# A two-layer graph network in Strassen-Winograd form: taller bank fills, smaller first sums, P2's first steps ahead of P6, and more of the next P1 inside the first aggregation

## The chip, the cores and the metric

The kernel runs on one core of a Trainium2 chip, in float32. The metric is the device time of one execution in microseconds (us): 1880.43 us, the median of three runs (1879.48 to 1881.2). One further execution was profiled; its span is 1878.8 us. The engines are called by the profile's names: PE is TensorE (PEld its weight loads), DVE VectorE, ACT ScalarE, POOL GpSimd, SP the engine that starts the DMAs.

## The reference

There are 64 graphs of N = 256 nodes with F = 512 features, a dense adjacency matrix for each, and weights that all graphs share.

```python
# layer 0
deg = sum(adj, -1);  agg = (adj @ x) / max(deg, 1e-6)
x1  = layernorm(x + relu(concat([x, agg], 2) @ W.T))
# layer 1
q, k = split(x1 @ Wqk);  v = x1 @ Wv
w   = inv_scale * mask * rowsum(q * (adj @ (k * mask)))
out = layernorm(x1 + softmax(w over nodes) * v)
```

In layer 1 the two halves of Wqk are multiplied with each other once, at the start, since rowsum(q * (adj @ k)) can be written as a row sum of (x1 @ (Wq Wk^T)) * (adj @ x1). So each layer is one product of the features with a 512 x 1024 weight and one product of an adjacency with a 256 x 512 matrix.

## The kernel before

**Pairs and layers.** Graphs are handled two at a time (index k), in 32 pairs. Loop index j runs over the pairs; iteration j holds layer 0 of pair j and layer 1 of pair j-1, written into each other. For iteration 0 there is no layer 1, and a tail after the loop does layer 1 of the last pair.

**Winograd's form of Strassen's product.** A feature-by-weight product is cut into 2 x 2 blocks and done with seven products instead of eight: P1 to P7, on sums S1 to S4 of the left blocks and T1 to T4 of the weight blocks. P4, P6 and P7 are plain products of 512 columns (`outer`, `pairs`); P1, P2, P3 and P5 are cut once more (`inner`), into seven products of 256 columns. `inner` returns four units: `first_two`, `second`, `third`, `last_two`. Their products share a working bank `w`: the upper half holds the fifth product, the lower half is accumulated on, and between products ScalarE copies what has been reached so far into the result banks. So `second` starts with a product onto `lo`, which `first_two` has accumulated and which `act.copy(q[0][:, :HF], lo)` has to read before. P1 and P2 use one working bank (`pw[0]`), P5 and P3 the other (`pw[1]`). P1 and P6 share the result banks `u`: when P1's four units are done, VectorE adds the fifth product to both banks, `after_p1` has ScalarE copy both to `own`, and P6 then accumulates on top in the same banks.

**Aggregation.** `gather` does the adjacency product as seven block products for both graphs, as units named a to g, on sums of adjacency blocks (`sa`, by GpSimd) and of feature blocks (`tv`, by VectorE).

**What sets the order.** Nothing is reordered later: matmuls, DMAs and the calls on VectorE, ScalarE and GpSimd go out in the order in which the program makes them. The order of the matmuls is written out by hand, in strings such as `run("i k i k", i=i, k=k)`; every letter takes the next unit of its list. In layer 0, i is P1, k is P5, m is P2, p is P6, q is P7, r is P3 and s is P4. After most units `tick()` looks at chains of queued vector and scalar steps (degrees, norms, softmax, weight sums) and issues those that are due by a small cost model: `mm` adds 0.43 or 0.86 us to a clock, and each engine has an estimate of when it is free.

**Start.** Eight products of a constant `ones` write each of the eight banks once (`fill`). Then follow 16 products for Wq Wk^T, while the weights and the first pair's features land, VectorE forms the weight sums and GpSimd the first `inner_sums`.

In the profile nearly all matmuls have line L175 (`mm`), all vector, scalar and GpSimd calls L90 (`InOrder`), all DMA starts L180; they are told apart by their tiles. `xT` holds layer 0's features turned, `xT_s` and `xT_i` their outer and inner sums, `x1T` those of layer 1; `t`, `t_i` and `w` are weight sums and weights; `bank` is a PSUM bank.

Of the kernel before, what the change touches and what calls it, by code (L numbers as in the profile page):

```python
# [36 lines left out]
BF16 = mybir.dt.bfloat16  # L37
# [4 lines left out]
P = 128  # L42
# [5 lines left out]
S1, S2, S3, S4 = range(4)  # L48
# [46 lines left out]
def resnorm_kernel(  # L95
# [13 lines left out]
    B, N, F = x.shape  # L109
# [8 lines left out]
    const = ctx.enter_context(tc.tile_pool(name="const", bufs=1))  # L118
# [49 lines left out]
    def run(order, **units):  # L168
        for name in order.split():
            units[name].pop(0)()  # L170
# [63 lines left out]
    wide = [const.tile([P, Q], F32, name=f"wide{k}") for k in (0, 1)]  # L234
    for w in wide:
        vec.memset(w, 0.0)
    ones = const.tile([1, P], BF16, name="ones")
    vec.memset(ones, 1.0)

    def fill(pair):  # L240
        for k in range(2):
            mm(pair[k].rearrange("p (a n) -> p a n", n=P), ones,
               ones[:, None, :].to_broadcast([1, F // P, P]), start=True)
    for pair in banks:
        fill(pair)

    def weight_product(c, ps):
# [49 lines left out]
    def inner_sums(X, eng, part):  # L297

        if X.s is None:
            X.open_sums()  # L300
        of_sum = lambda n: lambda k, e: X.s[:, k, X.slot[n]:X.slot[n] + 1, e]
        ks, b = ((slice(0, 2), X.first_row), (slice(2, 3), of_sum(S1)), (slice(0, 1), of_sum(S4)))[part]
        a11, a12, a21, a22 = (b(k, e) for k in range(2) for e in range(2))
        i = [X.i[:, r, ks] for r in range(4)]
        for to, op, c, d in ((i[0], OP.add, a21, a22), (i[1], OP.subtract, i[0], a11),
                             (i[2], OP.subtract, a11, a21), (i[3], OP.subtract, a12, i[1])):
            eng.tensor_tensor(to, c, d, op=op)
# [435 lines left out]
    for part in (work[:5], [sums[0][1]], work[5:10], [sums[1][1]], work[11:16]):  # L743
        for do in part:
            do()
    inner_sums(Xs[0], gp, 0)
    inner_sums(Xs[0], gp, 1)
    sumsA[0] = adj_sums(0)
    degrees(0)
    vec.free = clock[0] + 5.5  # L750
# [6 lines left out]
    early = []  # L757

    for j in range(NP):
        X = Xs.pop(j)  # L760
        if j == 2:
            steady.append(True)
        flush("finish")
        owns[j] = pool.tile([P, 2, NT, F], F32, name="own", bufs=3)
        if j > 0:
            load_adj(j)
            run_now(late_sums)
            late_sums.clear()
            sumsA[j] = adj_sums(j)

        u, y, o = pf, py, pu
        ys[j] = pool.tile([P, 2, NT, F], F32, name="y")
        a1, a2, a3, a4, a5, a6, a7 = layer0(j, o, u, y)
        i = inner("P1", X, W0, pw[0], u, a1)
        k = inner("P5", X, W0, pw[1], y, a5)
        m = inner("P2", X, W0, pw[0], o, a2)
        p, q = pairs(u, X, S2, W0["T2"], a6), pairs(u, X, S3, W0["T3"], a7)
        r, s = inner("P3", X, W0, pw[1], y, a3), pairs(u, X, A22, W0["T4"], a4)
        if j == 0:
            run("i k i k i k i k", i=i, k=k)  # L780
            flush("degrees")
            load_rows(1)
        elif j == 1:
            early.append(a1)
            run("k i k m k i k", i=early[0], k=k, m=m)
            fourth_sums(X, [1])
            run("m p p", m=m, p=p)
            fourth_sums(X, [0])
            run("p p m", m=m, p=p)
            load_x(1)  # L790
        else:
            run("i k", i=i, k=k)
            send_scores(j - 2)
            run("i l k", i=i, k=k, l=open1)
            flush("norm")
            fetch_scores(j - 2)
            places[0](range(16))
            run("i k i k", i=i, k=k)
        if j != 1:
            fourth_sums(X, [1])  # L800
        if j > 1:
            flush("mask")
            sumsM[j - 1] = adj_sums(j - 1)
            if j + 1 < NP:
                load_rows(j + 1)
            load_x(j)
        if j > 1:
            softmax(j - 2)
            shared[0] = 1.0
        if j != 1:  # L810
            run("m p p", m=m, p=p)
            fourth_sums(X, [0])
            run("m p p m", m=m, p=p)
        flush("w0a")
        run("q q q", q=q)
        flush("w0")
        run("r q r m", m=m, q=q, r=r)
        if j == 1:
            flush("norm")
        quiet[0] = j < 2  # L820
        room[vec] = -9.0 if j > 1 else 0.6
        run("r s r", r=r, s=s)
        if j > 0:
            Y = x1Ts.pop(j - 1)
        if j > 1:
            inner_sums(Y, gp, 0)
            queue(1, "sums", *outer_sums(Y, vec), (vec, lambda Y=Y: inner_sums(Y, gp, 1)))
        T_late = []
        T = sums_T(ys[j], T_late, 0 if j < 2 else 1)

        if j == 0:
            degrees(1)
        zs[j] = pool.tile([P, 2, NT, HF], F32, name="z")
        g = gather(sumsA.pop(j), T, zs[j], pw[1], y[1], y[0], owns[j], rdegs[j], T_late)

        def sums_next():
            if j == NP - 1:
                return
            inner_sums(Xs[j + 1], gp, 0)
            rest = outer_sums(Xs[j + 1], gp)  # L840
            run_now(rest[:1])
            inner_sums(Xs[j + 1], gp, 1)
            late_sums.extend(rest[1:])
        if j == 0:
            sums_next()
            held = [c for c in chains if c[1] == "w1"]
            chains[:] = [c for c in chains if c[1] != "w1"]
            early.append(inner("P1", Xs[1], W0, pw[0], u, lambda fifth: early[1](fifth)))
            run("s s a b s c d i e i g f", s=s, i=early[0], **g)
            quiet[0] = False  # L850
        else:
            u2, o2, y2 = o, pf, y
            b1, b2, b3, b4, b5, b6, b7, b8 = layer1(j - 1, ys[j][:, :, 0], o2, u2, y2)
            jj = inner("P1", Y, W1, pw[0], u2)
            k = inner("P2", Y, W1, y[0], o2, b2)
            if j == 1:
                turn_here(Y, owns[0], 0, pw)
                flush("mask")
                sumsM[0] = adj_sums(0)
                load_rows(2)  # L860
                run("s", s=s)
                turn_here(Y, owns[0], 1, pw)
                inner_sums(Y, gp, 0)
                sums_Y = (*outer_sums(Y, vec), (vec, lambda: inner_sums(Y, gp, 1)))
                run("s a b s d c", s=s, **g)
                quiet[0] = False
                flush("w1")
                run("e j g f", j=jj, **g)
                queue(1, "sums", *sums_Y)
                run("k j k j k j", j=jj, k=k)  # L870
                b1(None)
                run("k", k=k)
            else:
                run("s s j s a b", s=s, j=jj, k=k, **g)
                room[vec] = 0.6
                run("j", j=jj)
                if j < NP - 1:
                    degrees(j + 1)
                run("c d j k e j", s=s, j=jj, k=k, **g)
                quiet[0] = True  # L880
                run("k", k=k)
                quiet[0] = False
                b1(None)
                run("g f", **g)
        flush("softmax", "adds", "sums", "degrees")
        if j > 0:
            aggs[j - 1] = late.tile([P, 2 * N_SIDE], F32, name="agg").rearrange(
                "p (k t f) -> p k t f", k=2, t=NT)
            vs[j - 1] = [late.tile([P, NT, F], F32, name="v", bufs=2) for _ in range(2)]
            T = sums_T(owns[j - 1])  # L890
            g = gather(sumsM.pop(j - 1), T, aggs[j - 1], pw[0], o2[1], o2[0])
            h, q = pairs(u2, Y, S2, W1["T2"], b6), pairs(u2, Y, S3, W1["T3"], b7)
            n = inner("P5", Y, W1, pw[1], y2, b5)
            p, open1 = pairs(u2, Y, A22, W1["T4"], b4), inner("P3", Y, W1, pw[1], y2, b3)
            norm0(j)
            mask_adj(j)
            run("k h h" if j > 1 else "h h", k=k, h=h)
            if j == 1:
                degrees(2)
                flush("degrees")  # L900
            if j < NP - 1:
                load_xT(j + 1)
            run("n k h h" if j > 1 else "n h h", k=k, n=n, h=h)
            fourth_sums(Y)
            shared[0] = 1.25
            sums_next()
            run("a n b q d q n c q e q n p g f", n=n, q=q, p=p, **g)
            b8()
            run("p l p l p l", p=p, l=open1)
            py, pu = pu, py  # L910
        else:
            norm0(0)
            mask_adj(0)
            chains.extend(held)
# [113 lines left out]
```

## Time and profile before

| what | value |
|---|---|
| median of three runs | 1880.43 us |
| profiled span | 1878.8 us |
| PEld busy | 1314.0 us (70%) |
| POOL busy | 909.2 us (48%) |
| DMA | 181.27 MB, mean 96 GB/s |
| matmul 128x512, typical row | 592 ns |
| matmul 128x256, typical row | 380 ns |
| ACT copy of 128x256, 128x512 | 377, 583 ns |

The busy time of an engine is the union of its instructions' times. A float32 matmul shows as two records. Rows of consecutive matmuls overlap[...]; the distance between starts, and not a row's length, is what a matmul costs. In a timeline row the numbers are the start and the length in us; "x4" joins four like records, and "[0.26 <-X]" means that the engine was idle for 0.26 us before, and that X is inferred to have ended it.

### The profile page before, as it was taken

What the parts mean: (1) busy time and instruction counts of PE and PEld (TensorE: products, weight loads), DVE (VectorE), ACT (ScalarE), POOL (GpSimd) and SP (SyncE); (2) the same over time, 40 slices, a digit from 0 to 9 for tenths busy, and PEclk for the clock granted to TensorE, in tenths of its full rate; (3) what the DMA queues carried; (4) which work ended last, traced back from release to release, by engine and by line L of the source; (5) the groups of instructions that cost most, each with busy time, mean ns of one, the idle gap of its engine ahead of it and who ended that gap; (6) DMA issues with size and microseconds to landing.
All of it is one profiled execution on the core that took longest, in us unless ns stands there. A gap on an engine that the chain in (4) does not pass through costs nothing.

```text
span 1878.8 us, 25005 instructions
## 1 busy us (share of the span) xinstructions
PE 1859.2 (99%) x7000; PEld 1314.0 (70%) x7000; DVE 1511.1 (80%) x3180; ACT 1309.1 (70%) x3274; POOL 909.2 (48%) x1251
## 2 busy tenths in 40 slices
PE   9999999999999999999999999999999999999997
PEld 5667777767777677677677777776776777776765
DVE  6787888778887778887778887788877788877887
ACT  3667776677777677767777766777676777767766
POOL 4455443555444554535554535554445544355532
PEclk9999999999999999999999999999999999999999
DMA  6123334333333433343333334333434233433321
GB/s 225 57 69 82 100 94 113 90 90 96 107 97 88 114 82 99 90 118 85 100 91 103 96 98 106 85 99 96 110 85 113 80 103 94 110 94 86 99 64 51
DMA packets 380714, 181.27 MB, mean 96 GB/s; under 512 B 263712, under 2 KB 345248, under 8 KB 380576
## 3 DMA queue, kind: packets, MB, share of 16 engines
q1 hardware_dynamic: 380576, 179.67, 35.4%
q8 instruction: 57, 0.93, 0.2%
q14 instruction: 81, 0.66, 0.1%
HBM read 114.10 MB, written 34.06 MB: 79 GB/s over the span
## 4 chain that ended last, share of the span: by engine, by line
PE 96%; DVE 2%; ACT 1%; DMA 0%; issue 0%; POOL 0%; DVEq 0%; ACTq 0%
PE bank L175 96%; ACT own L90 1%; DVE v L90 0%; DVE own L90 0%; ACT bank L90 0%; DVE turn L90 0%; DMA wqk<-wqk_t 0%; DVE tv L90 0%; DVE y L90 0%; PE bank L628 0%; POOL xT_s L90 0%; DVE bank L90 0%; POOL sa L90 0%; ACT x1T L90 0%; DVE st L90 0%
## 5 line engine op out<-in xcount | busy, mean ns | idle before, releaser
L90 ACT COPY bank<-bank 128x256 f32<-128x256 f32 (+1 forms) x768 | 332.3, 435 | 235.8 <-PE bank L175 224.7
L90 DVE TENSOR_TENSOR y<-bank,y 128x512 f32<-128x512 f32 x256 | 170.5, 686 | 131.9 <-ACT y L90 131.3
L90 ACT ACTIVATE own<-own,shift,rstd 128x512 f32<-128x512 f32 x255 | 199.8, 808 | 0.9 <-DVE shift L90 0.9
L175 PE MATMUL bank<-tv,sa 128*128 128x256 f32 x768 | 192.5, 380 | 1.0 <-DVE tv L90 0.9
L90 POOL TENSOR_TENSOR x1T_s<-x1T,x1T_s 128x256 f32<-128x256 f32 x64 | 63.6, 1013 | 267.7 <-PE bank L175 267.7
L90 POOL TENSOR_TENSOR x1T_i<-x1T_s 128x128 f32<-128x128 f32 x128 | 101.1, 790 | 182.8 <-DVE x1T_s L90 182.8
L90 ACT ACTIVATE junk<-own,less 128x512 bf16<-128x512 f32 x254 | 183.7, 723 | 3.0 <-DVE less L90 2.1
L175 PEld LDWEIGHTS bank<-tv,sa 128*128 128x128 f32 x768 | 145.4, 190 | 49.9 <-issue 23.1
L90 ACT COPY y<-bank 128x512 f32<-128x512 f32 x192 | 108.8, 583 | 95.2 <-PE bank L175 93.7
L90 POOL TENSOR_TENSOR sa<-adj 128x256 f32<-128x256 f32 x128 | 94.7, 740 | 165.9 <-DMA adj<-adj_t 152.1
L175 PE MATMUL bank<-w,x1T_s 128*128 128x512 f32 (+1 forms) x384 | 168.3, 521 | 0.0
L90 POOL TENSOR_TENSOR x1T_i<-x1T 128x256 f32<-128x256 f32 x64 | 55.4, 866 | 221.6 <-DMA x1T<-turn 209.0
L175 PE MATMUL bank<-t,xT_s 128*128 128x512 f32 (+1 forms) x384 | 159.3, 524 | 2.5 <-ACT own L90 1.5
L175 PE MATMUL bank<-t,x1T_s 128*128 128x512 f32 (+1 forms) x384 | 158.1, 521 | 0.3 <-ACT y L90 0.3
L90 DVE TENSOR_TENSOR v<-bank,v 128x512 f32<-128x512 f32 x186 | 119.2, 682 | 48.8 <-PE bank L175 48.8
L175 PE MATMUL bank<-w,xT_s 128*128 128x512 f32 (+1 forms) x384 | 153.1, 521 | 0.0
L175 PE MATMUL bank<-t_i,xT_i 128*128 128x256 f32 x512 | 152.7, 380 | 0.3 <-DVE own L90 0.2
L175 PE MATMUL bank<-t_i,x1T_i 128*128 128x256 f32 x512 | 152.2, 379 | 0.1
L175 PEld LDWEIGHTS bank<-t_i,x1T_i 128*128 128x128 f32 x512 | 97.1, 190 | 67.1 <-issue 48.6
L175 PEld LDWEIGHTS bank<-t_i,xT_i 128*128 128x128 f32 x512 | 94.6, 189 | 58.2 <-issue 45.7
L90 ACT COPY own<-bank 128x512 f32<-128x512 f32 x128 | 71.8, 587 | 89.9 <-PE bank L175 49.3
L175 PE MATMUL bank<-t,x1T 128*128 128x512 f32 x256 | 130.4, 592 | 0.0
(159 smaller groups left out, 4565.6 us busy)
## 6 DMA issues: line engine op xcount, KB each, us to landing
x<-x SPq DMA_DIRECT2D x64, 512.0 KB, 5.7
xT<-x_t SPq DMA_DIRECT2D x62, 512.0 KB, 5.5
out<-own SPq DMA_DIRECT2D x62, 512.0 KB, 3.2
x1T<-turn SPq DMA_DIRECT2D x480, 64.0 KB, 2.3
adj<-adj_t SPq DMA_DIRECT2D x64, 256.0 KB, 3.8
turn<-adj SPq DMA_DIRECT2D x64, 256.0 KB, 3.0
row<-d SPq DMA_DIRECT2D x31, 256.0 KB, 4.7
wqk<-wqk_t SPq DMA_DIRECT2D x4, 512.0 KB, 5.7
```

The costliest lines, as they stand in the source:

```text
L90: return self.tc.keep_in_program_order(getattr(self.engine, name)(out, *args, **kwargs))
L175: tc.keep_in_program_order(nc.tensor.matmul(ps, a, b, start=start, stop=True, skip_group_check=True))
```

## The change

Five edits:

- The constant has 128 rows instead of one, so the fill products contract over all 128 rows, and the first two banks are filled twice: ten products instead of eight.
- `inner_sums` learns two more parts: those of P1 and of P2 alone. At the start GpSimd forms P1's sums, then P5's, then P2's, where it formed P1's and P2's together and then P5's.
- In layer 0 of pair 0 and of pairs 2 to 31, P2's first unit moves ahead of P5's last, and P2's second comes before P6 begins, its third between P6's two halves: from `i k i k i k i k | m p p | m p p m` to `i k i k i k i m k | m p p | m p p`.
- Three units of pair 1's P1, instead of two, run inside pair 0's aggregation; pair 1's own order changes to `k i k m k p k | p m | p p m`.
- In pair 1's iteration, aggregation unit b comes before a.

```diff
-    ones = const.tile([1, P], BF16, name="ones")
+    ones = const.tile([P, P], BF16, name="ones")
     vec.memset(ones, 1.0)
 
     def fill(pair):
         for k in range(2):
             mm(pair[k].rearrange("p (a n) -> p a n", n=P), ones,
-               ones[:, None, :].to_broadcast([1, F // P, P]), start=True)
-    for pair in banks:
+               ones[:, None, :].to_broadcast([P, F // P, P]), start=True)
+    for pair in (banks[0], *banks):
         fill(pair)
...
-        ks, b = ((slice(0, 2), X.first_row), (slice(2, 3), of_sum(S1)), (slice(0, 1), of_sum(S4)))[part]
+        ks, b = ((slice(0, 2), X.first_row), (slice(2, 3), of_sum(S1)), (slice(0, 1), of_sum(S4)),
+                 *((slice(v, v + 1), lambda k, e, v=v: X.first_row(k, e)[:, v:v + 1]) for v in range(2)))[part]
...
-    inner_sums(Xs[0], gp, 0)
-    inner_sums(Xs[0], gp, 1)
+    for part in (3, 1, 4):
+        inner_sums(Xs[0], gp, part)
...
         if j == 0:
-            run("i k i k i k i k", i=i, k=k)
+            run("i k i k i k i m k", i=i, k=k, m=m)
             flush("degrees")
             load_rows(1)
         elif j == 1:
             early.append(a1)
-            run("k i k m k i k", i=early[0], k=k, m=m)
+            run("k i k m k p k", i=early[0], k=k, m=m, p=p)
             fourth_sums(X, [1])
-            run("m p p", m=m, p=p)
+            run("p m", m=m, p=p)
             fourth_sums(X, [0])
             run("p p m", m=m, p=p)
...
-            run("i k i k", i=i, k=k)
+            run("i k i m k", i=i, k=k, m=m)
...
         if j != 1:
             run("m p p", m=m, p=p)
             fourth_sums(X, [0])
-            run("m p p m", m=m, p=p)
+            run("m p p", m=m, p=p)
...
-            run("s s a b s c d i e i g f", s=s, i=early[0], **g)
+            run("s s a b s c i d i e i g f", s=s, i=early[0], **g)
...
-                run("s a b s d c", s=s, **g)
+                run("s b a s d c", s=s, **g)
```

## The prediction

> **What bounds the kernel now.** I read the page first (busy shares and the chain that ended last), then the chain in order of time to find where it leaves TensorE, then the timeline around those places.
>
> ```profile
> PE 1859.2 (99%) x7000; PEld 1314.0 (70%) x7000; DVE 1511.1 (80%) x3180; ACT 1309.1 (70%) x3274; POOL 909.2 (48%) x1251
> PE 96%; DVE 2%; ACT 1%; DMA 0%; issue 0%; POOL 0%; DVEq 0%; ACTq 0%
> ```
>
> TensorE is 99% busy and 96% of the chain. All of its matmuls stay in the changed kernel, so a change can only move the time that TensorE stands still. That time comes from start-to-start distances: undisturbed, a 256-column record follows after 0.215 us and a 512-column one after 0.43 us, and whatever is longer is lost. Outside the first 95 us nothing much is lost. Two pairs show the place that the change rearranges in all 30 pairs from the third on. Columns are start, length, engine, line, operation, out<-in, shape, count.
>
> ```profile
> 1093.16 1.30 DVE L90 STREAM_TRANSPOSE turn<-own 128x512 f32<-128x512 f32 x2
> ...
> 1094.38 1.40 DVE L90 TENSOR_TENSOR bank<-bank,fifth 128x256 f32<-128x256 f32 x4
> ...
> 1094.69 0.59 PE L175 MATMUL bank<-w,xT 128*128 128x256 f32 x2
> ...
> 1094.82 1.07 ACT L90 COPY own<-bank 128x512 f32<-128x512 f32 x2 [1.65 <-DVE bank L90]
> ...
> 1095.55 1.95 PE L175 MATMUL bank<-t,xT_s 128*128 128x512 f32 x4 [0.26 <-POOL sa L90]
> ...
> 1095.77 0.39 ACT L90 COPY bank<-bank 128x256 f32<-128x256 f32 x1
> ```
>
> ```profile
> 350.69 1.50 DVE L90 TENSOR_TENSOR bank<-bank,fifth 128x256 f32<-128x256 f32 x4
> ...
> 351.12 1.07 ACT L90 COPY own<-bank 128x512 f32<-128x512 f32 x2 [1.07 <-DVE bank L90]
> ...
> 351.58 0.59 PE L175 MATMUL bank<-w,xT 128*128 128x256 f32 x2
> ...
> 352.01 1.88 PE L175 MATMUL bank<-t,xT_s 128*128 128x512 f32 x4
> ...
> 352.21 0.36 ACT L90 COPY bank<-bank 128x256 f32<-128x256 f32 x1
> ```
>
> When P1 ends, VectorE adds the fifth product to P1's two banks, ScalarE copies both banks to own, and P6 (t,xT_s, 512 columns) may then accumulate in the first of them. The releaser printed for P6 is POOL, but those subtractions do not touch its operands; the own copy, 0.15 us after whose end P6 starts, is what it needs. Its undisturbed start is 0.43 us after the row "w,xT", so 1094.69+0.43 = 1095.12, and 0.43 us are lost. In the second pair it starts on time. Over the 30 pairs, 14 lose 0.08 to 0.43 us, 3.8 us together, and the record after a wait comes 0.075 us late each time (14 x 0.075 = 1.05): 4.8 us in all. That is the most that hiding P6's wait can bring.
>
> The start and the first two pairs:
>
> ```profile
> 1.15 3.59 PE L175 MATMUL bank<-ones 1*128 1x512 bf16 x8 [1.15 <-DVE ones L90]
> 5.22 1.22 PE L175 MATMUL bank<-wqk 128*128 128x512 f32 x1 [0.47 <-DMA wqk<-wqk_t]
> 9.65 0.34 PEld L175 LDWEIGHTS bank<-wqk 128*128 128x128 f32 x1 [0.52 <-issue]
> 10.50 0.20 PEld L175 LDWEIGHTS bank<-wqk 128*128 128x128 f32 x1 [0.52 <-issue]
> 10.95 0.19 PEld L175 LDWEIGHTS bank<-wqk 128*128 128x128 f32 x1 [0.24 <-issue]
> 48.36 1.13 PE L175 MATMUL bank<-tv,sa 128*128 128x256 f32 x4 [0.90 <-DVE tv L90]
> 61.63 1.10 PE L175 MATMUL bank<-t,xT_s 128*128 128x512 f32 x2 [0.82 <-ACT own L90]
> 79.29 1.99 PE L175 MATMUL bank<-y,adj 128*128 128x256 f32 x8 [0.78 <-ACT x1T L90]
> ```
>
> Until 10.5 us the weight products come 0.85 us apart, afterwards 0.43 us apart: TensorE runs at half speed, although the clock column says full.
>
> **What the Trainium skill says.** "TensorE: Matmul & The Clock Gate", section "What's actually happening", has the array at half clock by default and at full clock after about 3.4 us of sustained activity, in windows that do not start with the kernel. The trace agrees on the factor (0.85 against 0.43 us); that eight one-row products over 3.6 us did not release the clock fits, but whether for their height or the pause of 0.47 us after them no run here shows. The same page, "LDWEIGHTS (loading the stationary operand)", makes the load's time depend on columns, not rows, so taller fill products cost nothing each. "PSUM — Partial Sum Buffer", section "Engine vs sequencer instructions", says that ScalarE and VectorE queues are strict FIFO and matmuls run in program order; in both pairs above ScalarE takes own, own, bank in issue order.
>
> **The change, part by part.**
>
> *Fill.* Two more products, all with 128 rows. Cold fill products stand 0.43 us apart, so ten last from 1.15 to 5.42 us and the first weight product moves from 5.22 to about 5.4: 0.2 us lost. TensorE is then active without a break from 1.15 us. If a clock window counts that was not counted before, the step at 10.5 us comes 3.4 us (the skill's window) earlier, and half of it is gained: 1.7. Ends: a loss of 0.2 if height and pause don't matter, a gain of 2.4 if all six slow steps (6 x 0.425 = 2.55) go. I take a gain of 1.5. It carries through: VectorE stood idle for 1.2 us before P1's adds at 27.8, waiting for TensorE.
>
> *First sums product by product.* POOL does twelve 128x128 operations instead of four 128x256 and four 128x128. The old four took 0.72+1.05+1.70+0.90 = 4.37, the small ones 0.67 each: eight for four is +1.0 us on POOL, behind which the sa sums wait, which TensorE first needs near 46. P1's and P5's sums are ready earlier than at 21.7, where ScalarE's copy of the weight product decides. I count 0 (bounds -0.3 and +0.3).
>
> *P2 ahead of P6, pairs 3 to 32.* The order at P1's end was: P1 last, P5 last, P2 first, P6. It is now: P1 last, P2 first, P5 last, P2 second, P6. The work between P1's end and the instruction that can wait stays the same, 4 matmuls of 0.43 us; but the one that stands there is now P2's second. It accumulates onto the lower half of the working bank, which P2's first has to be copied out of. On ScalarE that copy (bank<-bank, 128x256) stands in the issue order behind both own copies, as before, since P1's last unit still issues them first. So TensorE waits not for the first own copy but for own, own and bank. From the rows: own starts at s, the bank copy at s+0.95 (1095.77-1094.82), takes 0.39, and TensorE follows 0.14 later, as P6 did: s+1.48. Behind P2's second stand P6 and all else on TensorE; nothing can pass.
> - Pairs that wait today: 1094.82+1.48 = 1096.30 against 1095.12 is 1.18 us lost where 0.43 was: +0.75.
> - Pairs that don't: 351.12+1.48 = 352.60 against 352.01 is 0.59, plus 0.075 for the restart: +0.66. (In the trace the bank copy ran at 352.21 because P2's first ended then; it will be ready 0.86 us earlier and run at 352.07.)
> - Sum: 14 x 0.75 + 16 x 0.66 = 10.5 + 10.6 = +21.1 us. P6 itself then never waits, as the own copies are long done.
> P5's two adds move 0.86 us back on VectorE; the wait's own length covers that. ScalarE's softmax exponentials move behind P2's copies, POOL's and SP's orders here stay as they were, so DMAs do too. Bounds: every pair like the quick one, 30 x 0.66 - 4.8 = +15; every pair delayed like the mean of today's 14 (s 0.43 later, 1.09 each), 30 x 1.09 - 4.8 = +28.
>
> *First two pairs.* Pair 1 gets the same new wait (own starts at 28.24, P6's time 29.23): 28.24+1.48-29.23 = +0.5. Next pair's first P1 unit (2 x 0.43) now stands where 0.9 us were lost at 48.36: -0.8. In pair 2, P1's end is followed by 2.15 us of work instead of 1.29 before P6: -0.7 of the loss at 61.63. Taking the product into the other bank first at 79.29, where a copy of x1T is awaited: -0.7. Together -1.7 (bounds +0.5, as VectorE's chain of sums may hold the same end, and -2.5).
>
> **Sum.** 21.1 - 1.5 - 1.7 = +17.9 on the profiled span: 1878.8 + 17.9 = 1896.7. The median of the runs lies 1.6 above that span, so 1880.43 + 17.9 = 1898.3 us.
>
> **Rivals.**
> - *The pause lets the others catch up* (0.15). If VectorE's transposes are out of the way, as extra time per pair may do, its adds start with P1's end, own starts 0.2 us before the quick pair's, and the loss is 0.4+0.075 per pair: 30 x 0.47 - 4.8 - 3.2 = +6: 1886.5. For: VectorE is idle 20%. Against: the transposes follow matmuls of the same pair at a fixed distance.
> - *More pairs delayed* (0.12). VectorE's adds are late wherever a preceding row such as v<-v,fifth took longer; if that hits all pairs, +28 - 3.2: 1905.
> - *It does what its words say* (0.05). If the bank copy is done when P2's second comes up, P6's waits go and nothing takes their place: -4.8 - 3.2 = -8.0: 1872.4. It decides at s+1.48 before P6's undisturbed time; own would have to start 0.6 us earlier than in the quick pair, before P1's adds are through. Against it stand both rows.
> - *Gain and loss cancel* (0.02): that needs 18 us fewer losses than counted.
>
> **How the numbers follow.** The forecast has 0.66, the rivals 0.15, 0.12, 0.05 and 0.02. The range 1886 to 1906 takes in the forecast's bounds but for their tails, and the first two rivals. About 0.2% (3.8 us) is what a measurement here can tell from no change: faster 0.05, same 0.02, slower 0.93.
>
> **What would show it.** In the changed profile, pairs 3 to 32 lose 0.6 to 1.2 us before the second P2 product (t_i,xT_i after own, own, bank on ScalarE), P6 follows without a wait, and a pair takes about 0.7 us longer. The weight products reach 0.43 us near 7 us. I am wrong if those gaps are absent, or if the bank copy runs ahead of the own copies.

## The result and the profile after

The changed kernel is slower: 1904.87 us, the median of four runs (1904.53 to 1906.63), against 1880.41 us for the kernel before (four runs). The ratio is 1.0132 with a 95% interval of 1.0115 to 1.0150. The forecast was 1898.3 us with a range of 1886 to 1906. The profiled run of the changed kernel, 1904.9 us of span, is the slowest of its four (the other spans are 1902.7 to 1903.4).

The page of the changed kernel, busy times and the chain that ended last:

```profile
PE 1864.8 (98%) x7002; PEld 1314.7 (69%) x7002; DVE 1500.1 (79%) x3180; ACT 1306.3 (69%) x3274; POOL 914.8 (48%) x1255
PE 89%; DVE 5%; ACT 5%; issue 1%; DVEq 0%; ACTq 0%
```

TensorE's share of the chain falls from 96% to 89%; VectorE and ScalarE take what it lost. No engine's busy time grew by more than 6 us, so most of the loss is time in which TensorE stands still. Pairs are counted from 1 here, as in the prediction; the loop index j is one less. Where the time went is seen by setting the two traces beside each other, matmul by matmul (both have the same matmuls, apart from two more fill products), and taking the difference of the start times at the ends of three stages:

| stage | difference over the stage |
|---|---|
| start, up to the first P1 product | -2.24 us |
| pairs 1 and 2 | +6.47 us |
| pairs 3 to 32 | +21.83 us |
| sum | +26.06 us |

Pairs 3 to 32 first. The timeline around P1's end in two pairs of the changed kernel; the columns are start, length, engine, line, operation, out<-in, shape and count:

```profile
126.12 0.73 DVE L90 TENSOR_TENSOR bank<-bank,fifth 128x256 f32<-128x256 f32 x2
...
126.55 1.07 ACT L90 COPY own<-bank 128x512 f32<-128x512 f32 x2 [1.07 <-DVE bank L90]
...
127.01 0.59 PE L175 MATMUL bank<-t,xT_i 128*128 128x256 f32 x2
...
127.51 0.39 ACT L90 COPY bank<-bank 128x256 f32<-128x256 f32 x1
...
127.95 0.70 PE L175 MATMUL bank<-t_i,xT_i 128*128 128x256 f32 x2 [0.35 <-ACT bank L90]
...
128.49 1.88 PE L175 MATMUL bank<-t,xT_s 128*128 128x512 f32 x4
```

```profile
183.06 1.29 DVE L90 STREAM_TRANSPOSE turn<-own 128x512 f32<-128x512 f32 x2
...
184.28 0.73 DVE L90 TENSOR_TENSOR bank<-bank,fifth 128x256 f32<-128x256 f32 x2
...
184.71 1.07 ACT L90 COPY own<-bank 128x512 f32<-128x512 f32 x2 [1.56 <-DVE bank L90]
...
185.67 0.39 ACT L90 COPY bank<-bank 128x256 f32<-128x256 f32 x1
...
186.11 0.70 PE L175 MATMUL bank<-t_i,xT_i 128*128 128x256 f32 x2 [0.84 <-ACT bank L90]
```

ScalarE takes own, own, bank, and only then can TensorE begin P2's second product (t_i,xT_i). In the first pair it starts at 127.95 where 127.01+0.43 = 127.44 was possible: 0.51 us lost. In the second, where VectorE's transposes came later, it is 1.00 us. P6 (t,xT_s) follows without a wait. All 30 pairs have this gap, 0.51 to 1.21 us, 23.6 us in sum, and the record behind each is about 0.105 us late (3.1 us over the 30 pairs). Less the 4.8 us that P6 lost before, that is 26.7 - 4.8 = +21.9, against 21.83 in the table.

The start, and then the place in pair 2 that no step of the forecast had, both in the changed kernel:

```profile
1.17 4.45 PE L175 MATMUL bank<-ones 128*128 128x512 bf16 x10 [1.17 <-DVE ones L90]
5.41 14.19 PE L175 MATMUL bank<-wqk 128*128 128x512 f32 x32
6.13 0.19 PEld L175 LDWEIGHTS bank<-wqk 128*128 128x128 f32 x1 [0.38 <-issue]
6.56 0.19 PEld L175 LDWEIGHTS bank<-wqk 128*128 128x128 f32 x1 [0.24 <-issue]
19.46 0.67 PE L175 MATMUL bank<-t_i,xT_i 128*128 128x256 f32 x2
```

```profile
70.16 1.28 DVE L90 TENSOR_TENSOR own<-bank,own 128x512 f32<-128x512 f32 x2
70.20 1.02 PE L175 MATMUL bank<-t,agg 128*128 128x512 f32 x2
...
71.47 1.06 DVE L90 TENSOR_TENSOR own<-own,fifth 128x512 f32<-128x512 f32 x1
...
72.46 0.67 DVE L90 TENSOR_TENSOR shift<-less,rstd 128x2 f32<-128x2 f32 x1
...
73.17 1.52 ACT L90 ACTIVATE own<-own,shift,rstd 128x512 f32<-128x512 f32 x2 [2.79 <-DVE shift L90]
74.59 0.57 ACT L90 COPY bank<-bank 128x512 f32<-128x512 f32 x1
75.11 0.36 ACT L90 COPY fifth<-bank 128x256 f32<-128x256 f32 x1
75.22 1.22 PE L175 MATMUL bank<-t_i,xT_s 128*128 128x256 f32 x2 [3.99 <-ACT bank L90]
```

Weight products run at full speed, 0.43 us apart, from 6.1 us on, and the first P1 product starts at 19.46 us instead of 21.70. But from 71.1 us on TensorE stands still for 4.2 us, before P3's last unit (t_i,xT_s). Read upward: that unit waits for ScalarE's copies of P3's bank; they stand behind two scalings of pair 1's norm; the scalings wait for the small shift; and the shift, two values per partition, stands on VectorE behind the three adds of P2's result. In the kernel before, the shift and both scalings came ahead of those adds, and P3's last unit did not wait:

```profile
69.15 0.15 DVE L90 TENSOR_TENSOR shift<-less,rstd 128x2 f32<-128x2 f32 x1
...
70.98 0.82 ACT L90 ACTIVATE own<-own,shift,rstd 128x512 f32<-128x512 f32 x1
...
72.00 0.81 ACT L90 ACTIVATE own<-own,shift,rstd 128x512 f32<-128x512 f32 x1
...
72.52 1.28 DVE L90 TENSOR_TENSOR own<-bank,own 128x512 f32<-128x512 f32 x2
...
72.92 0.57 ACT L90 COPY bank<-bank 128x512 f32<-128x512 f32 x1
...
74.01 0.59 PE L175 MATMUL bank<-t_i,xT_s 128*128 128x256 f32 x2
```

Two queues in a row pass the delay on, and no single instruction in them takes longer than 1.1 us.

### The profile page after: what moved, and what is told of

It is laid out like the page before. It is cut to its first block, busy times and chain, and to the rows that moved or that the text cites. A ratio compares the mean times of both kernels' runs of the same rounds, so it can differ in the third digit from the quotient of the medians.

```text
span 1904.9 us, 25012 instructions
## 1 busy us (share of the span) xinstructions
PE 1864.8 (98%) x7002; PEld 1314.7 (69%) x7002; DVE 1500.1 (79%) x3180; ACT 1306.3 (69%) x3274; POOL 914.8 (48%) x1255
## 4 chain that ended last, share of the span: by engine, by line
PE 89%; DVE 5%; ACT 5%; issue 1%; DVEq 0%; ACTq 0%
PE bank L175 89%; ACT own L90 3%; DVE v L90 2%; ACT bank L90 1%; DVE turn L90 1%; DVE bank L90 1%; DVE own L90 1%; PE bank L629 0%; DVE st L90 0%; ACT y L90 0%; DVE tv L90 0%; PE bank L652 0%; DVE shift L90 0%; ACT junk L90 0%; DVE y L90 0%
## 5 line engine op out<-in xcount | busy, mean ns | idle before, releaser
L90 POOL TENSOR_TENSOR x1T_i<-x1T 128x256 f32<-128x256 f32 x64 | 63.5, 991 | 203.8 <-DMA x1T<-turn 182.9
```

The lines of the kernel that those rows point to most:

```text
L90: return self.tc.keep_in_program_order(getattr(self.engine, name)(out, *args, **kwargs))
```

## The experiments

Each ran against the kernel before on the same chip. Where the text says "at pair 3", it is the difference to the kernel before in the start of the same matmul, just after pair 2.

**Pairs 3 to 32 undone, and done alone.**

```diff
 e1: changed kernel
-            run("i k i m k", i=i, k=k, m=m)
+            run("i k i k", i=i, k=k)
...
-            run("m p p", m=m, p=p)
+            run("m p p m" if j else "m p p", m=m, p=p)
 e2: kernel before
-            run("i k i k", i=i, k=k)
+            run("i k i m k", i=i, k=k, m=m)
...
-            run("m p p m", m=m, p=p)
+            run("m p p" if j else "m p p m", m=m, p=p)
```

> The changed kernel, but pairs 3 to 32 have the old order around P2 and P6 (i k i k, then m p p, m p p m). Theory (the new wait of P2's second product costs 21.8 us from pair 3 on): about 1904.9 - 21.8 = 1883 us, pairs 3 to 32 as long as before, and still about 4 us behind at pair 3's start. Rival (the loss of later pairs is carried over from the long waits in the first two pairs, the other engines being late by then): the losses per pair stay, about 1900 us or more.

> The kernel before, with the new order around P2 and P6 in pairs 3 to 32 and nothing else. Theory: +21.8 us, about 1902 us, with 0.6 to 1.1 us lost before each second P2 product, and the first two pairs as before. Rival (carried over from the first two pairs): about 1880 us, within 4 us.

e1 measured 1884.47 us, a ratio of 1.0024 (1.0014 to 1.0034): +4.29 us at pair 3, and from there to the end +1.1, which is within what single traces differ by (see the fill runs below). e2 measured 1900.77 us, 1.0112 (1.0095 to 1.0129): -0.09 at pair 3, +20.5 from there to the end. So the order around P2 and P6 makes the loss of these pairs by itself, with an undisturbed start too, and nothing is carried over from pairs 1 and 2.

**The same order on TensorE, another on ScalarE.** The own copies are held back until P2's first unit has issued its bank copy (not in pair 2).

```diff
 e3: changed kernel
         def after_p1(fifth):
-            for k in range(2):
-                act.copy(own[:, k, 0], u[k])
+            def copies():
+                for k in range(2):
+                    act.copy(own[:, k, 0], u[k])
+            if j == 1:
+                copies()
+            else:
+                held_back.append(copies)
...
             act.copy(q[0][:, :HF], lo)
+            while p == "P2" and held_back:
+                held_back.pop(0)()
             tick()
```

> The changed kernel with TensorE's order untouched; on ScalarE alone the two own copies after P1 are issued after the bank copy of P2's first unit instead of before it (not in pair 2). Theory (TensorE waits for that copy because it is queued behind the own copies): the wait before P2's second goes, P6's wait is 0 to 0.15 us; pairs 3 to 32 take less time than before by some 3 to 4.8 us in sum, so about 1904.9 - 21.8 - 3.5 = 1879.5 us. Rival (what holds P2's second is its place on TensorE, close behind P2's first in the same bank): the wait stays near 0.6 us per pair, about 1897 us or more.

It measured 1878.90 us, 0.9993 (0.9985 to 1.0002). Pairs 3 to 32 took 4.4 us less than before; the gap is gone in all 30. The timeline of the pair that lost 1.00 us above:

```profile
182.06 0.73 DVE L90 TENSOR_TENSOR bank<-bank,fifth 128x256 f32<-128x256 f32 x2
...
182.35 0.36 ACT L90 COPY bank<-bank 128x256 f32<-128x256 f32 x1 [1.30 <-PE bank L175]
182.58 0.59 PE L175 MATMUL bank<-t,xT_i 128*128 128x256 f32 x2
182.62 1.08 ACT L90 COPY own<-bank 128x512 f32<-128x512 f32 x2
...
183.01 0.59 PE L175 MATMUL bank<-t_i,xT_i 128*128 128x256 f32 x2
...
183.44 1.88 PE L175 MATMUL bank<-t,xT_s 128*128 128x512 f32 x4
```

The bank copy runs at 182.35, in ScalarE's idle time before the own copies, which are hardly delayed by it (VectorE's two adds last until 182.79). P2's second starts 0.43 us after the row before it, P6 0.43 us after that. From pair 3 on the orders on TensorE, VectorE, GpSimd and the DMA queue are those of the changed kernel, and on ScalarE this one copy is all that moves (in pair 1 some steps of the degrees move as well). So the cause was the place of one copy in ScalarE's queue.

**Pair 2.** First its whole order was put back, with the third P1 unit out of pair 1's aggregation:

```diff
 e4: changed kernel
-            run("s s a b s c i d i e i g f", s=s, i=early[0], **g)
+            run("s s a b s c d i e i g f", s=s, i=early[0], **g)
...
-            run("k i k m k p k", i=early[0], k=k, m=m, p=p)
+            run("k i k m k i k", i=early[0], k=k, m=m)
...
-            run("p m", m=m, p=p)
+            run("m p p", m=m, p=p)
```

> The changed kernel with pair 2 as it was (two P1 units in pair 1's aggregation, pair 2's order k i k m k i k, m p p, p p m); aggregation unit b stays ahead of a, all else as changed. Theory (moving P1 and P6 in pair 2 shifts VectorE's second shift step of the norm behind P2's own adds, ScalarE's scalings and with them P3's bank copy wait for it, TensorE waits 4.2 us for that copy and then runs at half speed for a while): both gone, about 6.5 us less, 1898 us; pair 3 begins about 2 to 3 us earlier than in the kernel before. Rival (the wait comes of unit b going first, or of the two clocks of the planner being off through pair 1's order): the wait of about 4 us stays, 1904 us.

1900.32 us, 1.0108 (1.0093 to 1.0123). The difference at pair 3 is -1.71 us instead of +4.23, 5.9 us less, and the wait of 4.2 us is gone, with the half speed that follows it (last section). Then both mends together (e3's and e4's edits):

> Both mends together: the changed kernel with pair 2 as it was and the own copies issued after P2's first bank copy. Theory: start -2.2 us, pairs 1 and 2 about -1, pairs 3 to 32 about -3.5 against the kernel before: about 1873.5 us (1872 to 1877), faster than both. Rival (what is won at the start and at P6 is given back to VectorE or ScalarE elsewhere): 1880 us.

1874.02 us, the median of five runs (1873.73 to 1874.85), against 1881.41 us: a ratio of 0.9963 (0.9949 to 0.9976). -1.73 at pair 3, a further -4.0 after it. This version beats both kernels. Its page:

```profile
PE 1855.3 (99%) x7002; PEld 1312.8 (70%) x7002; DVE 1510.4 (81%) x3180; ACT 1304.7 (70%) x3274; POOL 911.7 (49%) x1255
```

To test the reading of the two queues, one run leaves pair 2's new order and moves the shift, and another brings the third P1 unit back alone:

```diff
 e6: e3's kernel
-        run("r q r m", m=m, q=q, r=r)
+        run("r q r", q=q, r=r)
         if j == 1:
             flush("norm")
+        run("m", m=m)
 e7: e5's kernel
-            run("s s a b s c d i e i g f", s=s, i=early[0], **g)
+            run("s s a b s c i d i e i g f", s=s, i=early[0], **g)
...
-            run("k i k m k i k", i=early[0], k=k, m=m)
+            run("k i k m k k", i=early[0], k=k, m=m)
```

> The copy-first kernel (pair 2 as in the changed one) with one more edit in pair 2: the steps still queued for pair 1's norm are issued before P2's last unit instead of after it, so that the second shift stands ahead of P2's three own adds on VectorE. TensorE's order is the same. Theory (the 4.2 us before P3's last product come from that shift standing behind the own adds): the wait falls by the adds' time, from 4.2 to about 1.7 us, and the run to about 1876.5 us. Rival (it is ScalarE's scalings themselves, or P3's bank copy, wherever the shift stands): the wait stays near 4 us, 1879 us.

> The kernel with both mends, with the third P1 unit back inside pair 1's aggregation; pair 2's order is otherwise the old one less that unit (k i k m k k, m p p, p p m), without P6's first product moved. In the issue order the second shift stands behind P2's own adds again. Theory: the third unit alone brings back the wait of about 4 us in pair 2 (and takes away about 0.8 us at the sums of pair 1's aggregation), so about 1874.0 + 4 = 1878 us. Rival (it was P6's first product, moved ahead of P5's last): no such wait, 1873 us.

e6 measured 1874.85 us, 0.9968 (0.9955 to 0.9980), -1.71 at pair 3. Its timeline at the same place:

```profile
69.31 0.15 DVE L90 TENSOR_TENSOR shift<-less,rstd 128x2 f32<-128x2 f32 x1
...
69.38 1.28 DVE L90 TENSOR_TENSOR own<-bank,own 128x512 f32<-128x512 f32 x2
69.50 1.52 ACT L90 ACTIVATE own<-own,shift,rstd 128x512 f32<-128x512 f32 x2 [0.77 <-DVE shift L90]
...
70.93 0.57 ACT L90 COPY bank<-bank 128x512 f32<-128x512 f32 x1
...
71.56 0.70 PE L175 MATMUL bank<-t_i,xT_s 128*128 128x256 f32 x2 [1.17 <-ACT bank L90]
```

The shift goes ahead of the own adds, the scalings start at once, and the loss before P3's last unit falls from 4.15 us in e3 to 1.34 us (a little less than the 1.7 expected; the scalings themselves remain in the way). So this version, too, beats both kernels. e7 measured 1878.65 us, 0.9988 (0.9981 to 0.9995), the median of 20 runs from 1876.56 to 1880.59: 2.2 us below the kernel before on the same chip, where e5 was 7.4 below. In its traced run (1877.26 us) the same unit loses 2.94 us and another 0.95 us is lost just before, so the third P1 unit alone brings most of the wait back. The last add and the shift take 0.69 and 0.15 us there instead of 1.06 and 0.67, which makes up 0.9 of the 1.2 us by which the two waits differ. It does take the loss of 1.06 us at the sums of pair 1's aggregation down to 0.21, as it was meant to, but gives more back in pair 2. Why that one unit lets the planner issue the shift so late was not tested.

**The fill.** Three runs of the kernel before, one execution each (1881.41 us for the unedited kernel on that chip): with ten products of 128 rows (f1), eight of 128 rows (f2), ten of one row (f3).

```diff
 f1, f2
-    ones = const.tile([1, P], BF16, name="ones")
+    ones = const.tile([P, P], BF16, name="ones")
...
-               ones[:, None, :].to_broadcast([1, F // P, P]), start=True)
+               ones[:, None, :].to_broadcast([P, F // P, P]), start=True)
 f1, f3
-    for pair in banks:
+    for pair in (banks[0], *banks):
```

> The kernel before with only the fill changed (ten products, 128 rows). The first P1 product should begin near 19.5 us instead of 21.7, as in the changed kernel; how much of the 2.2 us is left at pair 3 is open: 0 if VectorE's sums hold the first pair's end, 2 if not. So 1878 to 1880 us.

> The kernel before with eight fill products of 128 rows: the height without the two more. If height is what counts for the clock, full speed comes [...]near 5 to 8 us; if the pause before the weight products is what counts, the step stays at 9 to 12 us.

> The kernel before with ten fill products of one row: no pause before the weight products, but no height. If the pause is what counts, full speed near 5 to 8 us; if height, the step stays at 9 to 12 us and the weight products begin 0.2 us later.

They measured 1879.20, 1880.78 and 1882.51 us. Single times don't separate them: from pair 3 to the end, where none of the three has an edit, their traces moved by +0.2, +1.6 and +1.9 us against the kernel before. (The four traces with the copy moved, e3, e5, e6 and e7, gained 4.4, 4.0, 4.1 and 4.5 us there.) The start of the traces does separate them. Weight loads of the weight products, f2 and then f3:

```profile
4.98 0.30 PEld L175 LDWEIGHTS bank<-wqk 128*128 128x128 f32 x2 [1.12 <-DMA wqk<-wqk_t]
5.51 0.19 PEld L175 LDWEIGHTS bank<-wqk 128*128 128x128 f32 x1 [0.24 <-issue]
5.94 0.19 PEld L175 LDWEIGHTS bank<-wqk 128*128 128x128 f32 x1 [0.24 <-issue]
```

```profile
9.11 0.34 PEld L175 LDWEIGHTS bank<-wqk 128*128 128x128 f32 x1 [0.52 <-issue]
9.96 0.33 PEld L175 LDWEIGHTS bank<-wqk 128*128 128x128 f32 x1 [0.52 <-issue]
10.53 0.19 PEld L175 LDWEIGHTS bank<-wqk 128*128 128x128 f32 x1 [0.24 <-issue]
```

With eight tall products the distance is 0.43 us from 5.5 us on, in spite of the pause; with ten flat ones and no more than a short pause it is 0.85 us until 10 us. Height is what counts, and it costs nothing: ten tall products take 4.45 us in f1, ten flat ones 4.44 in f3. The two more products show no gain: the first P1 product begins 2.13 us earlier in f1 and 2.86 in f2, and at pair 3 the two are 1.53 and 1.41 us ahead, f3 0.01 behind. No run has the smaller first sums alone; the changed kernel, with them, starts its first P1 product at 19.46 us, and f1, without them, at 19.57.

## Why the prediction was right, and where it was not

*P2 ahead of P6.* Forecast +21.1 us, measured +21.8, and alone on the old kernel +20.5. The two pairs worked out in advance gave 0.59 and 1.18 us of loss, the measured gaps run from 0.51 to 1.21. That the cause is the bank copy behind the own copies is shown by e3, which moves nothing else in these pairs. The rival in which the pause lets the other engines catch up (0.47 us per pair) is refuted: 26.7 / 30 = 0.89 us per pair are lost in the changed kernel. The rival with more pairs delayed named 1905 us, which is the time measured, but not for its reason: it has +28 us in these pairs, and +21.8 came. "It does what its words say" came true only when the copy's place was changed with it: e3's 4.4 us are nearly all of the 4.8 that P6's waits were worth.

*Fill.* Forecast -1.5, measured -2.24 at the first P1 product; I had assumed that the step moves by one clock window, and it moved further. f1's -1.53 at pair 3 shows that about 0.6 us of such a gain is given back within pair 1, where P6 then waits (0.50 us in f1).

*First two pairs.* Forecast -1.7 with bounds of -2.5 and +0.5, measured +6.47: this step failed, in sign. Two of its terms were about right: the new wait in pair 1 (+0.5; the difference went from -2.24 to -1.70 us there) and the gap at the sums (-0.8; 1.06 us lost before, 0.20 after). The term for P6 in pair 2 (-0.7) had the wrong sign: P6 does not wait any more, but P5's third unit, which comes before it, waits for P5's bank copy behind the same two own copies. In the changed kernel:

```profile
55.62 1.07 ACT L90 COPY own<-bank 128x512 f32<-128x512 f32 x2 [1.67 <-DVE bank L90]
...
56.59 0.66 ACT L90 COPY bank<-bank 128x256 f32<-128x256 f32 x2
...
57.12 0.67 PE L175 MATMUL bank<-t,xT_i 128*128 128x256 f32 x2 [1.40 <-ACT bank L90]
```

1.56 us were lost there in place of 0.98: the mechanism that I had worked out for pairs 3 to 32, and did not look for in pair 2. The term of unit b before a (-0.7) came to nothing: in e4, which keeps that edit, the wait for x1T is gone, but 1.04 us are lost before the next sums (tv) where 0.94 had been lost. And the 4.2 us of pair 2 stood in no term, nor did the half speed behind them, which cost another 2.9 us (last section). The issue order of the changed kernel was known in advance and had the shift behind the own adds; I read it for pairs 3 to 32, where VectorE's order does not change, and not for pair 2, where it does.

*Sum.* The profiled span moved by 26.1 us, the median by 24.5, where 17.9 were forecast. The first two pairs account for all of the 8.2 us between them (6.47 + 1.7 = 8.2), since the errors of the start (-0.7) and of the later pairs (+0.7) cancel. That the time still lies in the range, 1.1 us below its upper end, is luck as far as the first two pairs go: the range was made wide for doubts about pairs 3 to 32, and it happened to take in this error too.

## What to carry to other kernels

When a matmul is moved to fill a wait, look for what *it* waits for, and where that stands in the queue of the engine that makes it: here a 0.39 us copy behind two others cost 22 us over 30 pairs, and moving the copy with the matmul turned the loss into a gain. On a kernel whose bound engine is 99% busy, follow each small step of the others through every queue that it passes; two values per partition, issued three instructions late, stopped TensorE for 4 us and left it slow for some more. Planned orders should be compared on all engines in the irregular first iterations too, not in the steady ones alone.

## What the runs showed of the hardware

Eight products of one row over 3.6 us did not raise TensorE's speed, eight of 128 rows did, with the weight products at the full rate 4.3 us after the first of them. All traces agree: in the nine with products of 128 rows the weight products stand 0.43 us apart from 5.4 to 7.0 us on, in the three with products of one row from 10.5 to 10.8 us on. The Trainium skill, "TensorE: Matmul & The Clock Gate", section "What's actually happening", speaks of how busy the engine is; the runs add that a busy row in the profile isn't enough.

The stop in pair 2 had an after-effect. Stages of the changed kernel, then one of e3, with busy times, the granted clock (after the busy times, 1.00 is full), and DMA:

```profile
72.00:75.00 3.00, 0.00 (x0) 0.00 (x0) 1.13 (x2) 1.83 (x3) 1.80 (x2) 0.87 0.00 0
75.00:79.00 4.00, 3.78 (x13) 3.32 (x14) 1.56 (x3) 1.06 (x3) 0.00 (x0) 0.50 0.00 0
```

```profile
75.00:78.00 3.00, 3.00 (x10) 2.53 (x11) 0.93 (x2) 0.29 (x2) 0.00 (x0) 0.50 0.00 0
```

After the stop of 4.15 us TensorE ran at half clock, and 256-column records came 0.43 us apart instead of 0.215. The granted clock of the changed kernel was 0.50 from 74.3 to 81.0 us, that of e1, with a stop of 4.16 us, from 74.4 to 81.1, that of e3, with one of 4.15, from 74.9 to 78.2 only. So the three traces with such a stop all show half clock behind it, but for 6.7 us in two and 3.3 in one. Against the kernel before, the changed kernel went from -2.95 to +1.20 us across the stop and on to +4.10 by the end of the half clock, e3 from -3.20 to +0.94 and on to +2.64. Behind the stop of 2.94 us in e7's trace the clock stayed at 1.00. e7's other executions have no trace: of the twenty, the eight with a mean granted clock of 0.996 took 1878.92 to 1880.59 us, the twelve with 0.997 took 1876.56 to 1878.84, so half clock after the stop in the eight would fit, but is not shown. Why the half clock lasts longer in some traces than in others was not tested. At the start of the kernel before, the same half speed (0.85 us between weight products) stood beside a clock column of 1.00; there the distances between starts are the better witness.
